# A decoder layer on one core: windowed cross scores on 32-row tiles of TensorE instead of 64-row tiles

## The chip, the cores and the metric

The kernel runs on one core of one Trainium2 chip, in one launch. The metric is the device time of that launch in microseconds (us), lower is better.

## The reference

One decoder layer for a batch of 32 sequences of 256 tokens, width 256, all in float32 at the interfaces. A self-attention, a windowed cross-attention and a quantised feed-forward follow each other, each with a residual and a layer norm:

```python
x = _layernorm(x + _L0_attn_ref(x, Wq, Wk, Wv, Wo))
x = _layernorm(x + _L0_xattn_ref(x, ctx, ctx, cell, ...))
x = _layernorm(x + _L0_ffn_ref(x, w_gate, w_up, w_down))
```

The self-attention has 16 query heads of 64 over 4 key and value heads, with rotary positions and an ALiBi bias. The feed-forward quantises activations to 8 bits and weights to three values. The change is in the cross-attention. It has 16 heads of 16 elements; queries and keys are layer-normed, projected and rotated; a query of a window of 64 sees the keys of its own window and of the one before it, if they are not later and lie in the same cell:

```python
p = jnp.einsum('bhnqd,bhnkd->bhnqk', bq, bk) / jnp.sqrt(hd)   # hd = 16
p = jnp.where(mask, p, finfo.min)
a = jax.nn.softmax(p, axis=-1)
o = jnp.einsum('bhnqk,bhnkd->bhnqd', a, bv)
```

So a query needs 128 scores for each head, each a sum over only 16 elements.

## The kernel before

**Staging.** The work of a batch element is cut into small functions and generators, and a hand-written schedule (the loop at the end of `tile_decoder_kernel`, L891 to L945) puts them into slots. A batch element has 16 slots of its own, two slots make a step, and later stages of one element run beside earlier stages of the next: while element b is in self-attention, b-1 is in cross-attention and b-2 in the feed-forward. TensorE, VectorE and ScalarE keep exactly the order in which the loop issues work; GpSimd and the DMA queue of SyncE are ordered by the framework. In each step TensorE does `self_turn` (L447, 8 transposes of probabilities of the step before), `cross_turn` (L693, transposes of cross probabilities), `self_scores` (L394) and, in every second step, `cross_scores` (L655); between them stand the projections (L331, L363, L604, L616), the value products (L464, L709), the output products (L495, L755) and the feed-forward (L802, L855).

**PSUM.** All matmul outputs come out of one pool of eight banks (L88). A function takes a bank by name (`bank("xs")`, `bank("t")`); a bank comes free when its last reader on VectorE or ScalarE is done.

**Cross keys and queries.** `cross_inputs` projects the keys of one batch element, transposed: 256 rows (16 heads of 16) by 256 keys, as two chunks `ch` of 128 partitions with eight heads each. GpSimd rotates them (L566 to L568), and eight DMAs on SyncE's queue copy them into `kTz` (L637 to L640). `kTz` has a slot `j` for each of the four heads of a half (64 partitions): head j's 16 rows go into slot j, and the rest of the slot stays at the zero that `prepare_buffers` wrote once (L169 to L170). One matmul with 64 rows of queries as weights and `kTz` as the moving operand (4 slots of 128 keys, 512 columns) so gives the scores of four heads, each in its own 128 columns of one bank.

**Cross scores.** A batch element has four calls of `cross_scores`, one for each query tile `qc` (128 queries) and chunk `ch`. For `qc` 0 a call is two matmuls, one for each half, on tiles of 64 rows by 128 columns of the array. For `qc` 1 the two windows of 64 queries see different keys (`spans`), so it is four matmuls, on tiles of 64 by 64. An f32 matmul leaves two records in the profile. VectorE then takes each head's 128 columns out of the bank, joins the mask and finds the maximum in one operation (L668, eight a call); ScalarE does the exponential (`cross_exp`, L684), TensorE the transposes (L693) and the value products (L709), and `cross_back` and `cross_output` the rest (L734, L755).

The prediction also names L420 (ScalarE's exponential of the self-attention, on `p`), L410 (VectorE's pass over the self scores `s`), L452 and L695 (ScalarE's copies out of the transposes), L471 (its copy of `o`), L816 and L817 (the gate of the feed-forward on ScalarE and VectorE), L206 (ScalarE's copy of a transposed layer norm, `zT`) and L550 (ScalarE's bias on projected queries, `qb`).

Of the kernel before, what the change touches and what calls it, by code (L numbers as in the profile page):

```python
# [9 lines left out]
F32 = mybir.dt.float32  # L10
# [6 lines left out]
P = 128  # L17
L = 256
NT = L // P
D = 256  # L20
NDC = D // P
# [7 lines left out]
XH, XHD, WINDOW = 16, 16, 64  # L29
XHH = 4  # L30
# [20 lines left out]
def kernel(  # L51
# [33 lines left out]
    def ctile(shape, dtype, name):  # L85
        return const.tile(shape, dtype, name=name, tag=name)
# [3 lines left out]
    def bank(name, shape=(P, 512), dtype=F32):  # L90
        return ps.tile(list(shape), dtype, tag="b", name=name)
# [12 lines left out]
    def work(name, shape, bufs=2, dtype=F32):  # L104
        return sb.tile(list(shape), dtype, tag=name, name=name, bufs=bufs)

    def small(name, n):
        return sb.tile([P, 8], F32, tag="small", name=name, bufs=48)[:, 0:n]
# [50 lines left out]
        t = ctile([P, (NT + 1) * XH * XE + 32 - XE], F32, f"xvaug{i}")  # L159
        xvaug_bufs.append(t)  # L160

    kTz = ctile([P, NDC, XHH, L], F32, "kTz")

    def prepare_buffers():
        nc.gpsimd.tensor_copy(cq_sb, cq_i)
# [8 lines left out]
    def stats(src, name):  # L174

        st = small("st", 6)
        mv = small(f"mv_{name}", 2)
        nc.vector.bn_stats(st, src)
        nc.vector.bn_aggr(mv, st)
        return mv  # L180

    def rstd_of(mv, name):

        rb = small(f"rstd_{name}", 2)
        nc.gpsimd.tensor_scalar(rb[:, 0:1], mv[:, 1:2], EPS, None, ALU.add)
        nc.gpsimd.tensor_tensor(rb[:, 0:1], rb[:, 0:1], neg_half[:, 0:1], ALU.pow)
        nc.gpsimd.tensor_scalar(rb[:, 1:2], mv[:, 0:1], rb[:, 0:1], -1.0, ALU.mult, ALU.mult)
        return rb
# [12 lines left out]
    def transposed(dst, src, name):  # L201

        pt = bank(name)
        for dc in range(NDC):
            nc.tensor.transpose(pt[:, dc * P : (dc + 1) * P], src[:, dc * P : (dc + 1) * P], ident)
        nc.scalar.copy(dst, pt[:, 0 : NDC * P].rearrange("p (c t) -> p c t", t=P))  # L206
# [338 lines left out]
    def biased(pq, j, n):  # L545


        qb = work("qb", [P, 2 * L])[:, 0 : NDC * n]
        for ch in range(NDC):
            nc.scalar.activation(  # L550
                qb[:, ch * n : (ch + 1) * n], pq[:, ch * n : (ch + 1) * n], AF.Identity, bias=xbcol[j][:, ch : ch + 1]
            )
        other = work("other", [P, 512], 3)[:, 0 : NDC * n]
        for e in range(2):
            nc.sync.dma_start(other[e : P : 2, :], qb[1 - e : P : 2, :])
        return qb, other

    def rotated(dst, qb, other, which, t0):

        n = dst.shape[2]  # L560
        q3 = qb.rearrange("p (c t) -> p c t", t=n)
        o3 = other.rearrange("p (c t) -> p c t", t=n)
        cos, sin = (
            rx_sb[:, which, i, t0 : t0 + n].unsqueeze(1).to_broadcast([P, NDC, n]) for i in range(2)
        )
        nc.gpsimd.tensor_tensor(q3, q3, cos, ALU.mult)  # L566
        nc.gpsimd.tensor_tensor(o3, o3, sin, ALU.mult)
        nc.gpsimd.tensor_tensor(dst, q3, o3, ALU.add)  # L568

    def cross_inputs(b):  # L570

        s = state[b]
        cs = work("cs", [P, NT, D], 1)
        nc.sync.dma_start(cs, cx[b].rearrange("(t p) d -> p t d", p=P))
        ck_i = work("ck_i", [P, L], 1, I32)
        nc.sync.dma_start(ck_i, cell_k[b].partition_broadcast(P))
        yield 4
        mvs = [stats(cs[:, t, :], "zc") for t in range(NT)]
        rstds = [rstd_of(mv, "zc") for mv in mvs]
        yield  # L580
        zc = cs
        for t in range(NT):
            last.append(partial(scaled, zc[:, t, :], cs[:, t, :], rstds[t]))
        ck = work("ck", [P, L], 1)
        nc.gpsimd.tensor_copy(ck, ck_i)
        yield 2
        zcT = work("tr", [P, NDC, L], 3)
        for t in range(NT):
            transposed(zcT[:, :, t * P : (t + 1) * P], zc[:, t, :], "zcT")


        s["mask"] = mask = work("mask", [P, NT, P])
        for rows_, t, k0 in ((slice(0, P), 0, 0), (slice(0, 64), 1, 64), (slice(64, P), 1, 128)):
            nc.gpsimd.tensor_scalar(
                mask[rows_, t, :], ck[rows_, k0 : k0 + P], cq_sb[rows_, b, t : t + 1], BIG, ALU.is_equal, ALU.mult
            )
        nc.gpsimd.tensor_tensor(mask, mask, base_sb, ALU.add)
        yield
        s["xv"] = xvaug_bufs[b % 2]
        xvaug = s["xv"][:, 0 : (NT + 1) * XH * XE].rearrange("p (t h e) -> p t h e", h=XH, e=XE)  # L600
        pk = bank("xk")
        for ch in range(NDC):
            for dc in range(NDC):
                nc.tensor.matmul(  # L604
                    pk[:, ch * L : (ch + 1) * L],
                    xkv_w[:, dc, ch * P : (ch + 1) * P],
                    zcT[:, dc, :],
                    start=(dc == 0),
                    stop=(dc == NDC - 1),
                )  # L610
        pair = biased(pk, K_, L)
        yield
        pv = bank("xv")
        for t in range(NT):
            for dc in range(NDC):
                nc.tensor.matmul(  # L616
                    pv[:, t * D : (t + 1) * D],
                    zcT[:, dc, t * P : (t + 1) * P],
                    xkv_w[:, dc, D : 2 * D],
                    start=(dc == 0),  # L620
                    stop=(dc == NDC - 1),
                )
        for t in range(NT):
            nc.vector.tensor_tensor(
                xvaug[:, t, :, 0:XHD],
                pv[:, t * D : (t + 1) * D].rearrange("p (h e) -> p h e", e=XHD),
                xbias[V_].rearrange("p (h e) -> p h e", e=XHD),
                ALU.add,
            )

        nc.sync.dma_start(xvaug[0:64, NT, :, :], xvaug[64:P, 0, :, :])
        nc.sync.dma_start(xvaug[64:P, NT, :, :], xvaug[0:64, 1, :, :])
        yield
        kT = work("tr", [P, NDC, L], 3)
        rotated(kT, *pair, 1, 0)
        yield 3
        for half in range(2):  # L637
            for j in range(XHH):
                rows_ = slice(half * 64 + j * XHD, half * 64 + (j + 1) * XHD)
                nc.sync.dma_start(kTz[rows_, :, j, :], kT[rows_, :, :])  # L640


# [5 lines left out]
    def cross_scores(b, i):  # L648
        s = state[b]
        qc, ch = cross_units[i]  # L650
        banks = [bank("xs") for _ in range(2)]
        for q0, q1, k0, _t in spans[qc]:
            for half in range(2):
                rows_ = slice(half * 64, (half + 1) * 64)
                nc.tensor.matmul(  # L655
                    banks[half].rearrange("p (h k) -> p h k", k=P)[q0:q1],
                    s["xqT", qc][rows_, ch, q0:q1],
                    kTz[rows_, ch, :, k0 : k0 + P],
                    start=True,
                    stop=True,  # L660
                )
        s["xnm", i] = [small("xnm", 4) for half in range(2)]
        for half in range(2):
            s["xp", i, half] = p = work("xp", [P, 512])
            for j in range(XHH):
                cols = slice(j * P, (j + 1) * P)

                nc.vector.tensor_tensor_reduce(  # L668
                    p[:, cols],
                    banks[half][:, cols],  # L670
                    s["mask"][:, qc, :],
                    -1.0,
                    3.0e38,
                    ALU.add,
                    ALU.min,
                    s["xnm", i][half][:, j : j + 1],
                )
# [203 lines left out]
    for b in range(B):  # L881
        s0 = 16 * b
        if b:
            at(s0 - 16, self_inputs(b))
        at(s0 + 2, cross_inputs(b))
        for t in range(NT):
            at(s0 + 2 * (5 + 4 * t), self_output(b, t))
            at(s0 + 2 * (CROSS + 5 + 4 * t) + 1, cross_output(b, t))
        at(s0 + 2 * (CROSS + 11) + 2, feed_forward(b))

    with tc.manual_schedule(engines={mybir.EngineType.PE, mybir.EngineType.DVE, mybir.EngineType.Activation}):  # L891
        running = []
        slot = min(starts)
        while starts or running:
            step, part = divmod(slot, 2)
            k, odd = divmod(step - CROSS, 2)
# [138 lines left out]
```

## Time and profile before

| | |
|---|---|
| median of 3 runs | 2324.79 us (2323.94 to 2325.04) |
| profiled execution | 2327.47 us |
| its span, first to last instruction | 2325.7 us |
| granted TensorE clock, mean | 0.987 |
| VectorE busy | 1701.3 us (73%) |
| ScalarE busy | 1764.8 us (76%) |
| GpSimd busy | 1124.2 us (48%) |
| weight loads of L655 | 768, 64\*64 and 64\*128 |
| L668 on VectorE, reading the scores | 1024 of 286 ns, 225.9 us |
| L640 on SyncE's queue, filling `kTz` | 256 DMAs of 32 KB, 2.0 us to landing |
| DMA, share of the 16 engines | 18.7% by the main queue |

In the profile PE is TensorE's matmul, PEld its weight loads, DVE VectorE, ACT ScalarE, POOL GpSimd and SP SyncE. A group names its line, engine, operation and tiles, then count, busy time and mean duration. "64\*128" is the tile of the array in rows and columns, "64x512" the moving operand. The duration of a matmul is its latency through the array, and matmuls overlap, so the rate of TensorE is read from the starts. The chain of waits is followed back from the last instruction: each piece either ran on an engine or was waited for. The page's shares of that chain for the lines named here: L331 12%, L394 10%, L495 10%, L447 8%, L464 8%, L693 4%, L655 4%.

### The profile page before, as it was taken

How to read it: one execution, taken by the hardware profiler on the slowest of the kernel's cores; microseconds unless marked ns; L12 is line 12 of the kernel's file. 1: busy time of each engine (PE TensorE's matmuls, PEld its weight loads, DVE VectorE, ACT ScalarE, POOL GpSimd, SP SyncE). 2: the span in 40 equal slices, each digit the busy share in tenths (PEclk: the TensorE clock that was granted, in tenths of full speed). 3: DMA queues.
4: the chain of work that ended last, by engine and by line, in shares of the span. 5: the costliest groups of instructions: out<-in, count | busy, mean ns of one | idle time of the engine just before them, and what ended most of it. 6: DMA issues, size and time to landing. Idle time of an engine off the chain costs nothing.

```text
span 2325.7 us, 54754 instructions
## 1 busy us (share of the span) xinstructions
PE 2246.9 (97%) x17637; PEld 1689.2 (73%) x17700; DVE 1701.3 (73%) x6949; ACT 1764.8 (76%) x5057; POOL 1124.2 (48%) x1851
## 2 busy tenths in 40 slices
PE   7999999999999999999999999999999999999985
PEld 5677777777777777777777777777777777777652
DVE  3767777777777777777777777777777777777765
ACT  2677777878777878777878777878777878777873
POOL 5344545445545545545445545445545444545432
PEclk9999999999999999999999999999999999999996
DMA  6311211112211111211111211112211111211000
GB/s 211 87 51 47 58 53 49 47 45 52 59 52 49 47 45 53 57 51 49 47 47 54 56 51 49 47 46 54 56 51 50 46 48 53 55 47 44 20 22 10
DMA packets 105407, 123.05 MB, mean 53 GB/s; under 512 B 21792, under 2 KB 74912, under 8 KB 105120
## 3 DMA queue, kind: packets, MB, share of 16 engines
q1 hardware_dynamic: 103424, 115.96, 18.7%
q10 hardware_dynamic: 1696, 3.57, 0.4%
q8 instruction: 142, 2.33, 0.4%
q14 instruction: 145, 1.19, 0.2%
HBM read 39.50 MB, written 8.39 MB: 21 GB/s over the span
## 4 chain that ended last, share of the span: by engine, by line
PE 78%; DVE 10%; ACT 8%; issue 1%; POOL 1%; DMA 1%; SPq 0%; ACTq 0%; POOLq 0%; DVEq 0%
PE proj L331 12%; PE s L394 10%; PE wo L495 10%; PE t L447 8%; PE o L464 8%; PE xt L693 4%; ACT p L420 4%; PE xs L655 4%; DVE gu L817 3%; PE xw L755 3%; PE xv L616 3%; PE ffo L855 3%; DVE p L410 2%; PE R L479 2%; PE xk L604 2%; PE v L363 2%
## 5 line engine op out<-in xcount | busy, mean ns | idle before, releaser
L420 ACT ACTIVATE p<-p,nm 128x256 f32<-128x256 f32 x1024 | 508.0, 498 | 168.6 <-DVE nm L410 164.7
L410 DVE CUSTOM_DVE_ANT_0 p<-s,alibi 128x256 f32<-128x256 f32 x1024 | 372.7, 420 | 180.5 <-PE s L394 180.4
L452 ACT COPY pT<-t 128x512 f32<-128x512 f32 x512 | 275.2, 591 | 127.1 <-PE t L447 126.8
L684 ACT ACTIVATE xp<-xp,xnm 128x128 f32<-128x128 f32 x1024 | 326.1, 394 | 5.9 <-DVE xnm L668 5.9
L394 PE MATMUL s<-kT,qT 64*128 64x256 f32 x2048 | 290.8, 402 | 0.0
L447 PE MATMUL t<-ident,p 128*128 128x128 f32 x2048 | 269.0, 273 | 3.2 <-ACT p L420 3.2
L447 PEld LDWEIGHTS t<-ident,p 128*128 128x128 f32 x2048 | 237.9, 141 | 31.4 <-ACT p L420 6.6
L331 PE MATMUL proj<-xT,wq_sb 128*128 128x256 f32 x1024 | 251.8, 389 | 0.0
L464 PE MATMUL o<-pT,v 128*64 128x256 f32 x2048 | 250.0, 385 | 0.0
L495 PE MATMUL wo<-wo_sb,oT 128*128 128x256 f32 x1024 | 245.3, 382 | 0.0
L668 DVE CUSTOM_DVE_ANT_0 xp<-xs,mask 128x128 f32<-128x128 f32 x1024 | 225.9, 286 | 2.9 <-PE xs L655 2.1
L495 PEld LDWEIGHTS wo<-wo_sb,oT 128*128 128x128 f32 x1024 | 189.4, 190 | 47.4 <-issue 22.7
L355 POOL TENSOR_TENSOR qT<-qT,other 128x512 f32<-128x512 f32 x128 | 162.9, 1273 | 120.6 <-DMA other<-psin 53.3
L394 PEld LDWEIGHTS s<-kT,qT 64*128 64x128 f32 x2048 | 176.5, 186 | 54.7 <-issue 23.5
L340 DVE TENSOR_TENSOR psin<-proj,rs_sb 128x512 f32<-128x512 f32 x160 | 110.2, 689 | 141.7 <-PE proj L331 141.7
L331 PEld LDWEIGHTS proj<-xT,wq_sb 128*128 128x128 f32 x1024 | 186.4, 191 | 32.8 <-issue 6.4
L464 PEld LDWEIGHTS o<-pT,v 128*64 128x64 f32 x2048 | 135.7, 136 | 98.3 <-issue 22.9
L420 ACT ACTIVATION_READ_ACCUMULATOR p<-p,nm 128x1 f32 x1024 | 192.6, 188 | 0.0
L695 ACT COPY xpT<-xt 128x512 f32<-128x512 f32 x256 | 153.2, 598 | 6.1 <-PE xt L693 4.2
L693 PE MATMUL xt<-ident,xp 128*128 128x128 f32 x1024 | 154.2, 274 | 0.0
L655 PE MATMUL xs<-kTz,xqT 64*64 64x512 f32 (+1 forms) x768 | 136.6, 611 | 5.0 <-POOL xqT L568 5.0
L817 DVE SCALAR_TENSOR_TENSOR gu<-gu,ff 128x512 f32<-128x512 f32 x128 | 82.3, 682 | 72.8 <-ACT gu L816 72.8
(156 smaller groups left out, 4528.2 us busy)
## 6 DMA issues: line engine op xcount, KB each, us to landing
other<-psin SPq DMA_DIRECT2D x640, 64.0 KB, 2.0
xT<-in_xt_dram SPq DMA_DIRECT2D x32, 256.0 KB, 2.7
xs<-in_x_dram SPq DMA_DIRECT2D x32, 256.0 KB, 2.7
cs<-in_ctx_dram SPq DMA_DIRECT2D x32, 256.0 KB, 2.7
other<-qb SPq DMA_DIRECT2D x64, 128.0 KB, 2.0
kTz<-tr SPq DMA_DIRECT2D x256, 32.0 KB, 2.0
other<-qb SPq DMA_DIRECT2D x128, 64.0 KB, 1.9
out_dram<-x SPq DMA_DIRECT2D x32, 256.0 KB, 2.2
```

Of the source, the lines that this page charges most:

```text
L331: nc.tensor.matmul(pq[:, c * L : (c + 1) * L], w[:, dc, c * P : (c + 1) * P], xT[:, dc, :], start=(dc == 0), stop=(dc == NDC - 1),)
L394: nc.tensor.matmul(banks[half][:, rr * L : (rr + 1) * L], qT[rows_, rr, qc * P : (qc + 1) * P], kT[rows_, kc, :], start=(rr == 0), stop=(r ...
L410: nc.vector.tensor_tensor_reduce(p[:, cols], banks[half][:, cols], alibi[:, 2 * (4 * kc + 2 * rp + rr) + half, :], -0.125, 3.0e38, ALU.add ...
L420: nc.scalar.activation(p[:, cols], p[:, cols], AF.Exp, bias=nm[:, rr : rr + 1], scale=-1.0, accum_out=s["sums", i // 2][:, (2 * rp + rr) * ...
L447: nc.tensor.transpose(pt[:, j * P : (j + 1) * P], p[half][:, rr * L + kk * P : rr * L + (kk + 1) * P], ident,)
L452: nc.scalar.copy(pT[half], pt)
L464: nc.tensor.matmul(po[half * HD : (half + 1) * HD, rp * L : (rp + 1) * L], s["v"][:, kk, (2 * kc + half) * HD : (2 * kc + half + 1) * HD], ...
L495: nc.tensor.matmul(py[:, 0:D], s["oT", qc, kc][:, r, :], wo_sb[:, 4 * kc + r, :], start=(kc == 0 and r == 0), stop=(kc == 1 and r == 3),)
L655: nc.tensor.matmul(banks[half].rearrange("p (h k) -> p h k", k=P)[q0:q1], s["xqT", qc][rows_, ch, q0:q1], kTz[rows_, ch, :, k0 : k0 + P], ...
L668: nc.vector.tensor_tensor_reduce(p[:, cols], banks[half][:, cols], s["mask"][:, qc, :], -1.0, 3.0e38, ALU.add, ALU.min, s["xnm", i][half][ ...
L684: nc.scalar.activation(p[:, cols], p[:, cols], AF.Exp, bias=s["xnm", i][half][:, j : j + 1], scale=-1.0)
L693: nc.tensor.transpose(pt[:, j * P : (j + 1) * P], p[:, j * P : (j + 1) * P], ident)
```

## The change

`kTz` keeps two slots instead of four. A tile is now 32 rows (two heads), and each of the four tiles of a chunk gets a PSUM bank of its own, of which it uses 256 of 512 columns. A call takes four banks instead of two and issues four matmuls of 256 columns for query tile 0 and eight for query tile 1, instead of two and four of 512 columns. The eight DMAs into `kTz` stay eight, of the same size; VectorE's eight reads a call stay, each out of another bank and column.

```diff
-    kTz = ctile([P, NDC, XHH, L], F32, "kTz")
+    kTz = ctile([P, NDC, 2, L], F32, "kTz")
...
-        for half in range(2):
-            for j in range(XHH):
-                rows_ = slice(half * 64 + j * XHD, half * 64 + (j + 1) * XHD)
+        for r in range(4):
+            for j in range(2):
+                rows_ = slice(r * 32 + j * XHD, r * 32 + (j + 1) * XHD)
                 nc.sync.dma_start(kTz[rows_, :, j, :], kT[rows_, :, :])
...
-        banks = [bank("xs") for _ in range(2)]
+
+        banks = [bank("xs") for _ in range(4)]
         for q0, q1, k0, _t in spans[qc]:
-            for half in range(2):
-                rows_ = slice(half * 64, (half + 1) * 64)
+            for r in range(4):
+                rows_ = slice(r * 32, (r + 1) * 32)
                 nc.tensor.matmul(
-                    banks[half].rearrange("p (h k) -> p h k", k=P)[q0:q1],
+                    banks[r][:, 0 : 2 * P].rearrange("p (h k) -> p h k", k=P)[q0:q1],
                     s["xqT", qc][rows_, ch, q0:q1],
                     kTz[rows_, ch, :, k0 : k0 + P],
                     start=True,
                     stop=True,
+                    tile_position=(r * 32, q0),
                 )
...
-                    banks[half][:, cols],
+                    banks[2 * half + j // 2][:, j % 2 * P : (j % 2 + 1) * P],
```

One line is added ahead of the matmul, so L655 is L656 in the changed kernel, and later lines move by two (L755 becomes L757).

## The prediction

> **What bounds the kernel now.** I read the page first (busy shares, chain by line, costly groups), then the chain of waits in order of time for one batch in mid-kernel, then the timeline of TensorE around the changed line, then the single records in it.
>
> The page: TensorE is busy 97% of the span, no other engine over 76%. The changed line is 4% of the chain that ended last, so about 93 us of it, although its 768 records last 611 ns each (470 us): tiles of the array overlap.
>
> ```profile
> PE 2246.9 (97%) x17637; PEld 1689.2 (73%) x17700; DVE 1701.3 (73%) x6949; ACT 1764.8 (76%) x5057; POOL 1124.2 (48%) x1851
> ...
> L655 PE MATMUL xs<-kTz,xqT 64*64 64x512 f32 (+1 forms) x768 | 136.6, 611 | 5.0 <-POOL xqT L568 5.0
> ```
>
> The chain in order of time (start us, us, what). A batch takes 69.65 us (1080.98 - 1011.33, the same call one batch on) and holds four calls of the cross scores: two for query tile 0 (64\*128 tiles, at 1011.33 and 1062.80) and two for query tile 1 (64\*64 tiles, at 1030.79 and 1047.56). Three are on the chain. The fourth is not: from 1040.90 to 1052.63 the chain runs through DVE and ACT, and TensorE is released by ACT's copy of zT.
>
> ```profile
> 1029.79 1.06 PE s L394 x8
> 1030.86 1.02 PE xs L655 x8
> 1031.88 1.92 PE xv L616 x8
> ...
> 1039.78 1.11 PE s L394 x8
> 1040.90 0.41 DVE p L410
> ...
> 1051.86 0.51 ACT qb L550 x2
> 1052.37 0.27 ACT zT L206
> 1052.63 0.04 issue
> 1052.67 1.13 PE xw L755 x4
> ...
> 1061.90 1.06 PE s L394 x8
> 1062.96 0.86 PE xs L655 x4
> 1063.82 1.92 PE wo L495 x8
> ```
>
> The timeline of TensorE gives starts; the durations are latencies, so I count from start to start. Both forms take 0.95 to 1.02 us, with 4 records or with 8.
>
> ```profile
> 1030.79 1.09 PE L655 MATMUL xs<-kTz,xqT 64*64 64x512 f32 x8
> 1031.81 0.70 PE L616 MATMUL xv<-xkv_w,tr 128*128 128x256 f32 x2
> ...
> 1062.80 1.02 PE L655 MATMUL xs<-kTz,xqT 64*128 64x512 f32 x4
> 1063.75 0.48 PE L495 MATMUL wo<-wo_sb,oT 128*128 128x256 f32 x1
> ```
>
> **Prices, from single records of that stretch.** Each f32 matmul leaves two records (two passes), each streaming its columns at about 0.833 ns: in L394 a pass of 256 columns is followed by the next on the same rows after 215 ns, in L655 one of 512 after 429. Tiles of other rows or columns start 6 to 7 ns apart and stream together (1030.787, .793, .800, .807). Where the tile size changes, the first start comes some 95 ns late (L693 to L394: 203 ns instead of 109), and the first load is no longer hidden: the first pass is longer by 105 ns for 128 weight columns, 53 for 64, 27 for 32 (L709).
>
> **What the Trainium skill says.** "TensorE: Matmul & The Clock Gate", section "Part 3: Packing small matmuls": tiles of distinct row groups run concurrently, with about 4 ns more per tile; the trace agrees for two row tiles and for a 2x2 grid, with 7 ns. It gives 3.07 times for four row tiles of 32; no run here shows four yet. "TensorEngine Tiling (Array Packing)", "Key Properties": a change of tiling mode drains TensorE; the trace agrees (95 ns). Same page, "Gotcha 1: PSUM Pressure": row tiles need banks of their own, hence four.
>
> **The change, part by part.**
>
> Matmuls of query tile 0. Before: 216 ns from the start of the last L394 pass to L655 (both 64\*128, no drain, weights preloaded), then 955 to the next line: 1171. After, the tile is 32\*128, so there is a drain: 215 + 98 = 313 (what the 64\*64 form shows now). First pass 213 + 107 for an exposed load, second pass 213 + 93 drain + 3 x 7 for the later tiles: 313 + 320 + 327 = 960. Saved 0.211 us a call.
>
> Matmuls of query tile 1. Before 313 + 1019 = 1332, all calls within 2 ns. After: 313, 213 + 53, 213 + 93 + 7 x 7: 934. Saved 0.398 us a call.
>
> On the path: 2 x 0.211 + 0.398 = 0.82 us a batch, x32 = 26.2 us. The fourth call's 0.4 us lies beside DVE and ACT, which work without a gap from L394 at 1039.78 to zT at 1052.63; it makes TensorE's 0.39 us wait at L755 about 0.8 and counts nothing. Batch 0 has no feed-forward beside its fourth call: 0.4 more. In the last batch the granted clock is down (the call at 2260.83 takes 2.05 us and is on the chain): some 0.6 more. Sum 27.2.
>
> Banks. Each call takes four of eight instead of two. The semaphore waits in the built order of the changed kernel say whose readers must be done; I set these against the times of before. In the three calls on the path the last release (an ACT copy of t or xt, or DVE's reading) stands 0.87, 0.69 and 0.60 us ahead of L655. In the fourth it is DVE's L817, ending 1047.59 against a start at 1047.56: up to 0.1 us, inside that call's spare 0.4. Behind a waiting xs matmul stand all later matmuls of the slot, and behind them DVE's softmax pass of the cross scores. Later users move too: in the calls on the path the nearest is xq, some 0.5 us, of which 0.2 is used up by the earlier arrival; xv keeps 1.2 - 0.4. Cost taken: 0; at worst 0.1 us x 96 = 10.
>
> More instructions. 384 more matmuls; each new one is one more 7 ns start, counted. 105 more semaphore instructions on PE at 51 ns (5.4 us if none is covered): PE's queue runs ahead over half a us where all waits are met, so 0 to 5; I take 0. DVE's 1024 reads keep form and number (286 ns each), only in other banks: 0.
>
> kTz. The same 8 DMAs of 32 KB a batch, in the same place on SP; issued from 1048.7 to 1054.3 and landing 2.0 to 3.6 us later, they are done by 1058, 4.9 us ahead of 1062.8. SP gets 62 more semaphore instructions in all, covered by these 4.9 us. The clearing of kTz halves (two of 952 ns on POOL at 17 to 20 us), where the chain waits on weight DMAs: 0.
>
> Sum against the profiled execution: span 2325.7 - 27.2 = 2298.5, with its 1.8 us around, 2300.3. It is 2.7 us over the median of the runs; 2324.79 - 27.2 = 2297.6, **forecast 2298**.
>
> **Rivals.**
> - *Slower: the four row tiles stream two at a time.* Nothing in this trace has four. A pass then stays 427 ns, and what remains is the new drain and load of query tile 0 (313 + 534 + 541 = 1388, +217 ns x 64 = 13.9 us) and 30 ns more in the third call (1 us): 2340. With a pass of w ns a batch gains 2(637 - 2w) + (824 - 2w) ns, so it decides from w = 350 on, under 2.44 tiles at a time (853 / 350). Against it: two row tiles overlap fully, and four column tiles in L709 start 7 ns apart. 8%.
> - *Four overlap in part.* At the skill's 3.07 times w is 278 (an estimate): 81 ns x 64 + 268 x 32 = 13.8 us, 2311. 8%; with a few us of bank and semaphore waits also between 2307 and 2320.
> - *The waits take the gain.* 96 calls of 0.27 us would do: 2318 to 2327. For it: half of all banks in one call. Against it: 0.6 us of margin at least. 5%.
> - *The fourth call counts too*, if the DVE and ACT stretch gets shorter by itself: 31 x 0.4 = 12 us, 2286. Against it: no idle time in that stretch. 6%.
>
> **How the numbers follow.** The forecast has 73% and its own range is 2293 to 2307 (10 us for banks or semaphores upward, 5 down for a cheaper drain or load: 96 x 0.05). 2290 to 2312 takes in the second rival's centre and leaves out the slower one, most of the third and the fourth, under 2 in 10. A measurement of this kernel tells about 0.2% (4.6 us) from no change. Faster: 73 + 8 + 6 and 2 of the third's 5, 0.89; same 0.03; slower 0.08.
>
> **What would show it.** Eight matmul records of the 32\*128 form starting 7 ns apart in two passes some 320 ns apart, start to start with the next line 0.65 us instead of 0.955; for 32\*64, 0.62 instead of 1.02. The share of L656 (the new number of L655) in the chain falls from 93 us to about 65. TensorE's wait on zT at L757 doubles from 17 us. A batch takes 68.8 us. I am wrong if passes stay 430 ns apart, if the last two xs matmuls start late behind ACT, or if TensorE gains idle time in the three calls on the path.

## The result, and the profile after

The changed kernel takes **2301.44 us** (median of 4 runs, 2301.18 to 2301.88) against 2324.65 for the kernel before (4 runs): a ratio of 0.990, 95% interval 0.988 to 0.991. That is 23.2 us faster; 27.2 were forecast, and the time lies inside the stated range of 2290 to 2312.

The page after: TensorE lost 30.8 us of busy time, the other engines nothing that matters.

```profile
PE 2216.1 (96%) x18468; PEld 1691.5 (74%) x18468; DVE 1698.8 (74%) x6949; ACT 1762.5 (77%) x5057; POOL 1124.7 (49%) x1851
```

The chain of waits after, in order of time, for the same stretch of a batch element (11.0 us earlier, because of the batches before it). The columns are start us, us, what.

```profile
1018.82 1.06 PE s L394 x8
1019.88 0.62 PE xs L656 x16
1020.50 1.93 PE xv L616 x8
...
1028.41 1.11 PE s L394 x8
1029.52 0.41 DVE p L410
...
1040.48 0.51 ACT qb L550 x2
1040.99 0.26 ACT zT L206
1041.26 0.04 issue
1041.30 1.13 PE xw L757 x4
...
1050.53 1.06 PE s L394 x8
1051.59 0.64 PE xs L656 x8
1052.23 1.92 PE wo L495 x8
```

The three calls on the chain shrank from 0.86, 0.86 and 1.02 us to 0.64, 0.64 and 0.62. The stretch from the scores (`s`) to `xw`, in which the chain runs through VectorE and ScalarE, is what it was: 1039.78 to 1052.67 before and 1028.41 to 1041.30 after, 12.89 us both times.

TensorE's timeline after, for the third, the fourth and the first call. In the brackets is the idle time before the group and what ended it.

```profile
1019.81 0.69 PE L656 MATMUL xs<-kTz,xqT 32*64 32x256 f32 x16
1020.43 1.99 PE L616 MATMUL xv<-xkv_w,tr 128*128 128x256 f32 x8
...
1036.19 0.74 PE L656 MATMUL xs<-kTz,xqT 32*64 32x256 f32 x16
1036.86 1.04 PE L804 MATMUL ff<-ff_up,xiT 128*128 128x512 bf16 x4
...
1041.30 1.13 PE L757 MATMUL xw<-xo_w,zT 128*128 128x256 f32 x4 [0.74 <-ACT zT L206]
...
1051.52 0.71 PE L656 MATMUL xs<-kTz,xqT 32*128 32x256 f32 x8
1052.16 1.99 PE L495 MATMUL wo<-wo_sb,oT 128*128 128x256 f32 x8
```

The fourth call (1036.19) is nearly as short as the third, 0.67 us to the next line against 0.62, and what it saves stands in the bracket further down: TensorE idles 0.74 us ahead of L757, where it idled 0.39 us before:

```profile
1052.67 1.13 PE L755 MATMUL xw<-xo_w,zT 128*128 128x256 f32 x4 [0.39 <-ACT zT L206]
```

Below, **the period** is the time from one batch element to the next (the first record of L363), median over the run's profile. In the steady part (from the fifth period to the last but one) it repeats to about 0.01 us, but for one or two longer batches in some kernels, and is much sharper than the medians of runs. It fell from 69.655 to 68.825 us, by 0.830; forecast were 0.82 and a period of 68.8.

### The profile page after: what moved, and what is told of

It reads as the page before. It is cut to its first block, busy times and chain, and to the rows that moved or that the text cites. A ratio compares the mean times of both kernels' runs of the same rounds, so it can differ in the third digit from the quotient of the medians.

```text
span 2299.6 us, 56520 instructions
## 1 busy us (share of the span) xinstructions
PE 2216.1 (96%) x18468; PEld 1691.5 (74%) x18468; DVE 1698.8 (74%) x6949; ACT 1762.5 (77%) x5057; POOL 1124.7 (49%) x1851
## 4 chain that ended last, share of the span: by engine, by line
PE 77%; DVE 10%; ACT 8%; issue 1%; DMA 1%; POOL 1%; SPq 0%; ACTq 0%; POOLq 0%; DVEq 0%
PE proj L331 12%; PE s L394 10%; PE wo L495 10%; PE t L447 8%; PE o L464 8%; PE xt L695 4%; ACT p L420 4%; DVE gu L819 3%; PE xw L757 3%; DVE p L410 3%; PE xs L656 3%; PE xv L616 3%; PE ffo L857 3%; PE R L479 2%; PE xk L604 2%; PE v L363 2%
## 5 line engine op out<-in xcount | busy, mean ns | idle before, releaser
L394 PE MATMUL s<-kT,qT 64*128 64x256 f32 x2048 | 290.4, 402 | 0.0
L331 PE MATMUL proj<-xT,wq_sb 128*128 128x256 f32 x1024 | 254.2, 392 | 0.0
L394 PEld LDWEIGHTS s<-kT,qT 64*128 64x128 f32 x2048 | 176.2, 186 | 54.4 <-issue 27.6
L331 PEld LDWEIGHTS proj<-xT,wq_sb 128*128 128x128 f32 x1024 | 188.2, 193 | 33.4 <-issue 6.9
L819 DVE SCALAR_TENSOR_TENSOR gu<-gu,ff 128x512 f32<-128x512 f32 x128 | 82.2, 682 | 72.8 <-ACT gu L818 72.8
L594 POOL TENSOR_SCALAR mask<-ck,cq_sb 64x128 f32<-64x128 f32 (+1 forms) x96 | 77.5, 807 | 114.1 <-DVE xnm L670 108.1
```

The costliest lines, as they stand in the source:

```text
L331: nc.tensor.matmul(pq[:, c * L : (c + 1) * L], w[:, dc, c * P : (c + 1) * P], xT[:, dc, :], start=(dc == 0), stop=(dc == NDC - 1),)
L394: nc.tensor.matmul(banks[half][:, rr * L : (rr + 1) * L], qT[rows_, rr, qc * P : (qc + 1) * P], kT[rows_, kc, :], start=(rr == 0), stop=(r ...
```

## The experiments

The runs of the kernel before that stand beside each experiment had medians from 2324.91 to 2325.28 us.

**One part of the change alone.** Three kernels keep the old `kTz` with four slots and use the 32-row tiles in some of the four calls of a batch element; they differ in the condition alone.

```diff
+        quarters = qc == 0        # or i == 2, or i == 3
-        banks = [bank("xs") for _ in range(2)]
+        banks = [bank("xs") for _ in range(4 if quarters else 2)]
...
-            for half in range(2):
-                rows_ = slice(half * 64, (half + 1) * 64)
+            for r in range(4 if quarters else 2):
+                n = 32 if quarters else 64
+                j0 = 2 * (r % 2) if quarters else 0
+                nj = 2 if quarters else 4
+                rows_ = slice(r * n, (r + 1) * n)
...
-                    kTz[rows_, ch, :, k0 : k0 + P],
+                    kTz[rows_, ch, j0 : j0 + nj, k0 : k0 + P],
```

Calls 1 and 2:

> Only the calls of query tile 0 (calls 1 and 2 of a batch element) use four 32-row tiles; kTz keeps four slots and a 32-row tile takes the two that hold its heads. Theory (the gain is TensorE time in the three calls on the chain): 64 calls x 0.214 us = 13.7 us, so 2311. Rival, the gain belongs to the smaller kTz or to all calls alike: no gain with the old layout (2325), or half of 23 us spread over four calls (2313, not to be told from the theory here).

Measured: 2314.59 us, ratio 0.9954 (0.9941 to 0.9966), period 69.231, that is 0.424 less, or 2 x 0.212. The median is 3.6 us above the 2311 expected and nearer to the rival's 2313; it can't tell the two apart. The period can, and the next two kernels rule out that all calls count alike.

The third call:

> Only the third call of a batch element (query tile 1, first chunk) uses 32-row tiles. Theory: 32 x 0.402 us = 12.9 us, so 2312. Rival, all calls count alike: a quarter of 23 us, 5.8, so 2319.

Measured: 2313.08 us, ratio 0.9951 (0.9938 to 0.9963), period 69.255, 0.400 less.

The fourth call, with the same edit:

> Only the fourth call of a batch element (query tile 1, second chunk) uses 32-row tiles: the same edit in TensorE as for the third call. Theory: hidden, TensorE waits on zT longer by what it saves; 0.4 us in batch 0 and some tenths in the last, so 2324 to 2325. Rivals: it counts like the third (2312), or its late bank, released by L817, costs more than it has spare (slower than 2325).

Measured: 2326.12 us, ratio 1.0005 (0.9999 to 1.0012), period 69.653: no gain. TensorE's waits on zT at L755's place in the whole run rise from 17.4 to 27.6 us, which is 31 x 0.33.

The three periods together give 0.826 of the 0.830 us. So the gain is a sum over calls; it doesn't come from the layout of `kTz`, which these kernels don't change; and the same edit is worth 0.400 us in the third call and nothing in the fourth.

**Four banks without 32-row tiles.** Each matmul is cut in two of 256 columns into banks of their own:

```diff
-        banks = [bank("xs") for _ in range(2)]
-        for q0, q1, k0, _t in spans[qc]:
-            for half in range(2):
-                rows_ = slice(half * 64, (half + 1) * 64)
+        banks = [bank("xs") for _ in range(4)]
+        for jj in range(2):
+            for q0, q1, k0, _t in spans[qc]:
+                for half in range(2):
+                    rows_ = slice(half * 64, (half + 1) * 64)
...
-                    kTz[rows_, ch, :, k0 : k0 + P],
+                        kTz[rows_, ch, 2 * jj : 2 * jj + 2, k0 : k0 + P],
```

> The old 64-row tiles and the old kTz, but a call's scores go into four banks, each matmul cut into two of 256 columns: twice the matmul and load records, the same columns. Theory: TensorE's columns set the time, banks cost nothing: 2325 to 2328 (some 20 ns a call for more records). Rival, four of eight banks in one call delay later users: over 2335. Rival, the gain came from VectorE getting its first scores earlier out of smaller banks: under 2318.

Measured: 2325.46 us, ratio 1.0001 (0.9993 to 1.0009), period 69.665, 0.01 more. Taking half of PSUM in one call costs nothing at the pace of before and gains nothing; nor do twice as many matmuls of half the columns. That leaves the rows of the tile: with 32 rows instead of 64, twice as many tiles share a pass, and a call is done in two passes of 256 columns instead of two of 512.

**The kernel before once more.**

> The kernel before, unchanged, profiled once more. The profiled execution of before took 2327.5, 2.7 us over the median; that of after lay on its median. If the 2.7 us are chance (weights' DMAs at the start, say), this profile shows a span near 2323 and the difference to the first sits in one place outside the steady part. If they are steady, the batch period differs from 69.65 us.

Measured: 2326.14 us in the profiled execution, span 2324.3, period 69.654. Against the first profile of before, batch 31 starts 1.2 us later and what follows its start is 2.5 us shorter (203.6 us against 206.1). The steady part is the same; the ends differ by some us from one execution to the next.

**The wait at the end of the hidden stretch.** In `cross_output` the product `xw` of the first query tile is issued one slot later, so that TensorE does the next step's transposes and scores ahead of it:

```diff
             transposed(zoT, on, "zoT")
-            yield
+            yield 2 if t == 0 else 1
```

> The changed kernel, and the output product of the first query tile (xw, one of two in a batch element) one slot later, so that TensorE does the next step's transposes and scores while ScalarE comes to zT. Theory (in the fourth call TensorE waits 0.74 us for zT): the wait goes, 31 x 0.74 = 23 us, so 2279. Rival, ScalarE and VectorE are the bound through the whole of the feed-forward stretch and the wait comes back at the next transposes: 2295 to 2302.

Measured, on the changed kernel: **2279.84 us**, ratio to before 0.9802 (0.9788 to 0.9815), period 68.164.

> The kernel before with the same move of xw. Theory: the wait of 0.39 us goes, 31 x 0.39 = 12 us, so 2313; with the run of the changed kernel and the same move, 32-row tiles are then worth 34 us instead of 23, because the fourth call counts. Rival, the wait comes back elsewhere: 2320 to 2325, and the tiles stay worth 23.

Measured, on the kernel before: 2304.21 us, ratio 0.9908 (0.9894 to 0.9921), period 69.000.

The move is worth more than expected on the kernel before (0.655 us a batch instead of 0.39) and less than expected on the changed one (0.661 instead of 0.74). That the median of the changed kernel agrees with the 2279 expected is luck: two errors nearly cancel. So the tiles are worth 69.000 - 68.164 = 0.836 us with the move and 0.830 without: the fourth call still counts nothing, and the expectation of 34 us for the tiles was wrong. Two things are behind it. First, this wait cost more than its idle time: `xw` takes 1.13 us on the chain after the wait and 0.86 when it follows other work, and 0.39 + 0.27 is the 0.66 measured. Second, a new wait took the fourth call's place. The timeline of weight loads of the changed kernel with the move:

```profile
1034.05 0.57 PEld L447 LDWEIGHTS t<-ident,p 128*128 128x128 f32 x4
1034.90 0.42 PEld L447 LDWEIGHTS t<-ident,p 128*128 128x128 f32 x4 [0.28 <-ACT qb L550]
```

The second half of the transposes `t` waits 0.28 us, and the profile names as releaser ScalarE's bias operation L550 (on `qb`), the last reader of the bank that these transposes need. From the start of `s` in the fourth call's slot to these transposes TensorE is 0.35 us faster than in the kernel before with the move, and `t` and `xr` (the transposes of `cross_back`) then take 0.35 us longer on the chain (1.44 against 1.09).

**Two attempts to take that wait away.** The first also moves the projection behind L550 one slot on (`yield 3` and `yield 1` for `yield 2` and `yield 2` around `xq` of the first query tile), on both kernels, and once with query tile 0 cut into 64 columns as described below.

> The changed kernel with xw one slot later, and the projection xq of the first query tile one slot later too, so that ScalarE's two bias operations (L550, 0.5 us) leave the queue ahead of the next transposes. In the run with xw alone moved, TensorE came 0.35 us early to these transposes (L447) and waited for the bank that L550 reads, so the fourth call was still worth nothing. Theory: this wait goes, 31 x 0.35 = 11 us, period 67.8, so 2269. Rival, ScalarE is behind by more than its two bias operations and the next operation in its queue takes the place: period 68.1, so 2278 to 2281.

> The kernel before with the same two moves. There TensorE waited for nothing more after the first move (period 69.00), so 2303 to 2305 under both theories. With the run of the changed kernel and the same two moves it gives what the tiles are worth when the fourth call counts: theory 1.2 us a batch (0.83 + 0.40), some 35 us; rival 0.84, some 24.

> The changed kernel with both moves and query tile 0 on tiles of 64 columns as well: 0.058 us a batch under the run with both moves alone (what that cut gave by itself), 1.8 us, so 2267 by the theory, 2277 by the rival.

Measured: 2289.79 us, period 68.533; 2313.30, period 69.366; 2288.66, period 68.48 (ratios 0.9847, 0.9951 and 0.9843, each within 0.0014). A miss: the second move costs 0.37 us on both kernels. With it the first transposes wait for ScalarE, now for the copy of `zT` and so for the bank of `zoT`, on the chain of the changed kernel with both moves:

```profile
1036.08 0.27 ACT zT L206
1036.35 0.04 issue
1036.39 1.09 PE t L447 x8
```

and L394 takes 1.33 us on the chain instead of 1.06, on both kernels; what delays L394 stays open.

The second attempt leaves all engines' order alone but ScalarE's, in the fourth call's slot:

```diff
-            if part == 1 and not odd:
+            if part == 1 and not odd and k % 4 < 3:
                 cross(cross_exp, k, 0)
...
                     cross(cross_values, k - 1)
+                    if k % 4 == 3:
+                        cross(cross_exp, k, 0)
```

> The changed kernel with xw one slot later (period 68.16), and one more edit in ScalarE's order alone: in the fourth call of a batch element its first four exponentials (L686) come after the bias operations, the copy of zT and the copy of xoT instead of ahead of them, so that the banks of xq, zoT and xo come free 1.2 us sooner. TensorE, VectorE, GpSimd and DMA keep their order. Theory (the fourth call's 0.40 us are lost because ScalarE holds the bank that L447 needs): the wait of 0.35 us goes, of which some 0.15 may come back at the value products (L464), which need ScalarE's copies of the transposes after all eight exponentials; period 67.8 to 68.0, so 2269 to 2275. Rival (ScalarE's whole work between the scores and those copies sets the time, whatever its order): period 68.16, so 2280.

Measured: **2275.33 us**, ratio to before 0.9785 (0.9772 to 0.9799), period 67.994. The chain of this kernel (the batch shown here comes later than those above):

```profile
1093.45 1.06 PE s L394 x8
1094.52 0.68 PE xs L656 x16
...
1098.83 0.87 PE t L447 x8
1099.70 0.22 PE xr L731 x2
...
1101.42 2.06 PE o L464 x16
```

`t` is back at 0.87 and `xr` at 0.22, no wait; `o` takes 2.06 instead of 1.88. So of the 0.35 us of this wait 0.17 (68.164 - 67.994) arrive, and 0.18 go to the value products, as expected. Whether they belong to the fourth call is argued, not shown: the kernel before was not run with this second edit. Its chain with `xw` moved alone has no such wait to lose (`t` 0.87, `xr` 0.22, `o` 1.88), so that a gain isn't to be expected there. It is the fastest kernel of the study.

**The weight load of query tile 0.** The changed kernel with two tiles of 64 columns for query tile 0 as well:

```diff
+    score_spans = {0: ((0, 64, 0, 0), (64, P, 0, 0)), 1: spans[1]}
...
-        for q0, q1, k0, _t in spans[qc]:
+        for q0, q1, k0, _t in score_spans[qc]:
```

> The changed kernel, with query tile 0 also cut into two tiles of 64 columns (eight matmuls of 256, as for query tile 1). Theory (the exposed first load costs columns / 1.2 ns, further tiles 7 ns): 957 -> 930 ns a call, 64 x 0.027 = 1.7 us, so 2299.7. Rival, more matmuls and waits cost more than the load saves: 2302 to 2306.

Measured: 2300.81 us, ratio to before 0.9891 (0.9878 to 0.9905), period 68.767, 0.058 less, or 2 x 0.029. From the last pass of `s` to the next line a call takes 930 to 933 ns instead of 957 to 959. The medians alone can't tell this from nothing; the period can.

## Why the prediction was right

- **The rate of four row tiles** was the open point, and the slower rival stood on it. The single records show four starts at 1051.521, .527, .534 and .541 and the next pass 320 ns after the first, as worked out (213 + 107). Four tiles stream at once, at no loss; a pass of 213 ns, not the 278 estimated from the 3.07 of the Trainium skill ("TensorE: Matmul & The Clock Gate", "Part 3: Packing small matmuls"). The kernel with four banks settles it without a sum: on its 64\*64 tiles the first pass of 256 columns in the third call lasts 267 ns, and on the 32\*64 tiles of the changed kernel 267 ns too.
- **The terms of a call.** 957 ns against 960 worked out for query tile 0, 930 against 934 for query tile 1. The new drain ahead of query tile 0 is there (313 ns instead of 216). One reading beside these terms was wrong and cost nothing: at 17 to 20 us the chain runs through the projections L331 and doesn't wait on weight DMAs; the clearing of `kTz` isn't on it.
- **The fourth call.** Hidden, as forecast, shown by the kernel with that call alone. The wait at L757 is 0.74 us, forecast about 0.8. But in the whole run it didn't double: it rose from 17.4 to 28.1 us, since some of the 17.4 us are longer waits in batch 0 and the last batches, which grow by 0.4 us at most, and since each fourth call gives back 58 ns to a late bank.
- **Banks.** No late start in the three calls on the path (all within 2 ns in the steady part). In the fourth the last tile starts late, as the waits had it: at 1036.259, just after VectorE's L819 (L817 before) ends at 1036.204; median 988 ns instead of 930. This costs nothing there. That row tiles need banks of their own was taken over in the prediction from the page that it names; no run here tries two in one bank.
- **The sum.** The steady part is right to 0.01 us a batch (0.830 against 0.82). The terms that were mis-sized are the count of batches and the ends. Not 32 batches gain 0.83 us: 27 of the 31 periods do, and the two ahead of them 0.73 and 0.61. From the start of batch 2 (counted from 0) to that of batch 31 this makes 23.7 us, near the 23.2 between the medians. The 0.4 us for batch 0 rested on no feed-forward running beside its fourth call. The call is hidden all the same: TensorE waits for `zT` there too, in the profile of before and then in that of the kernel with the fourth call alone:

```profile
149.49 1.13 PE L755 MATMUL xw<-xo_w,zT 128*128 128x256 f32 x4 [1.71 <-ACT zT L206]
149.37 1.13 PE L762 MATMUL xw<-xo_w,zT 128*128 128x256 f32 x4 [2.11 <-ACT zT L206]
```

The wait grows by the 0.40 us that the call saves. The 0.6 us for the last batch rested on the slow clock of one execution: the call at 2260.83 takes 2.05 us on the chain of the first profile of before, and 1.16 in the second. What such ends gain can't be seen: the two profiles of the kernel before differ by 1.3 us ahead of batch 2, and by 2.5 us from the start of batch 31 on (206.1 and 203.6 us; 204.1 after).

- **The rival in which the fourth call counts** didn't come about by itself. With `xw` moved the tiles are still worth no more than without; with four exponentials moved too, 0.17 us more, if the kernel before would neither gain nor lose by that second edit. ScalarE's order, and not the position of one product alone, decides in that stretch.

## What to carry to other kernels

Where small contractions fill only part of the array, count passes from start to start and add two prices for a tile shape of its own: the drain at the change of shape and the first weight load, which is no longer hidden. Cut the sum by what each call's slot lets through: the same edit was worth 0.40 us in one slot and nothing in another, and the chain of waits in order of time showed which before anything was run. Check that the chain is the same in the first and last batches before the sum is multiplied by all of them. Where a stretch is held by another engine, look at what TensorE waits for at its end, an operand or a PSUM bank, and at when that engine comes to it: here one product moved gained 0.66 us a batch and four exponentials another 0.17, together as much again as the tiles did (2301 to 2275 us).

## What the runs showed of the hardware

- Tiles of other rows or columns start 6 to 7 ns apart, for two, four and eight tiles, loads and matmuls alike, and four tiles of 32 rows stream as fast as two of 64: a first pass of 267 ns on both.
- Passes of 128, 256 and 512 columns on the same rows start 109, 215 and 429 ns apart. This is 0.833 ns a column ((429 - 109) / 384) and some 2 ns a pass.
- A change of tile shape cost 94 to 98 ns in the cases seen (128\*128 to 64\*128, 64\*128 to 64\*64 and to 32\*128), and the exposed first load some 107, 53 and 27 ns for 128, 64 and 32 weight columns, over a pass at 0.833 ns a column.
- A TensorE wait of 0.39 us cost 0.66: the group after it took 1.13 us on the chain instead of 0.86.
- Four of eight banks in one call instead of two, with twice as many matmuls, cost 0.01 us a batch. Where a bank came free late, it was the reader that mattered: VectorE's L819 held back a tile of the fourth call, and, with `xw` moved, ScalarE's L550 held back the transposes behind it.
